# A layer norm's multiply moved from VectorE to GpSimd in a selective-scan kernel on one core

## The chip, the cores and the metric

The kernel runs on one core of a Trainium2 chip. The metric is the device time of one execution in microseconds. Before the change it is 16063.91 us, the median of three runs (16063.67 to 16070.08). In the profile, PE is TensorE's matrix unit and PEld its weight loads, DVE is VectorE, ACT is ScalarE, POOL is GpSimd and SP is the queue that issues nearly all DMAs.

## What is computed

Two blocks follow each other on a float32 tensor of 32 images, 96 channels and 56 x 56 positions. The first is a depthwise 7 x 7 convolution, a norm over the channels, two dense layers with a GELU between them, and a residual. The second is a pair of selective-scan layers over the 3136 positions of an image, then a batch norm over all images. Cut to the core of one layer of the second block:

```python
mu = seq.mean(-1); var = ((seq - mu) ** 2).mean(-1)
h = (seq - mu) * rsqrt(var + EPS) * ln_g + ln_b
xs, z = split(h @ in_w)
xc = silu(sum(conv_w[:, k] * shifted(xs, k) for k in range(4)) + conv_b)
dt, Bm, Cm = split(xc @ xproj_w)
delta = softplus(dt @ dt_w + dt_b)
state[t] = exp(delta * A) * state[t-1] + delta * Bm * xc     # 192 channels x 16 states
y = sum_s(state * Cm) + Dp * xc
seq = seq + (y * silu(z)) @ out_w
```

The change concerns the second line: the product with 1/sqrt(var + EPS). The mean is taken out by the weights that are prepared once, so the product is formed from seq itself and one row of 1/sqrt per position, the same in all 96 partitions.

## The kernel before

The 3136 positions of an image are four chunks of 784, and a chunk of a layer is one stage: 32 x 4 x 2 = 256 stages. Layer 0 of chunk n+1 and layer 1 of chunk n alternate. A stage has 24 steps (`NSTEP`): six groups j of 32 channels x 4 states over the partitions, times four state groups g. Each step is one scan on VectorE over 784 or 785 positions (`scan`, L959). For four of the six groups (j = 0, 1, 3, 4) VectorE also multiplies the scan's input from u and B (`times_b`, L887), four products per group; for groups 2 and 5 GpSimd does it (`pooled`, L941). After every second scan GpSimd multiplies the two states by C (L964), and TensorE adds them up into y (`add_up`, L1005) with L997 for the D term. VectorE multiplies y by the gate z (`gate`, L980) three times a stage. ScalarE forms exp(delta * A) ahead of each scan (`exps`, L904 and L905), and copies the carried states (L973). TensorE spreads u over the partitions (`spread`, L931), with a few matmuls without use before it, set by `FILL` (`keep_warm`, L917).

Between the steps stand pieces of other work: preparing the next stage (`prep`), finishing the last (`post`), half a chunk of the first block for an image further on (`block0`), and convolution taps for a later image (`conv`, seven taps, L552). The order is written out by hand. Each piece has a slot number: its integer part is the step after whose scan it is put, counted from the stage's start, and the fraction orders the pieces of one step. A piece marked `True` goes ahead of the scan's own products instead. Every engine, and SP, executes its instructions in exactly the order that comes of this (`manual_schedule`); waits on other engines are put in where data or buffers demand them.

In `prep`, the norm of the next stage is made thus. TensorE centres the chunk in two halves of 392 (L371), ScalarE squares them (L376), TensorE takes the mean over the channels (L381), and ScalarE turns it into 1/sqrt by a logarithm and an exponential (`rsqrt`, L387 and L388), in place in PSUM. VectorE then multiplies seq by that row of PSUM into the halo tile `hn` (L611, `norm(a)`, once per half), which has one buffer per layer and three columns of the previous chunk ahead of the 784 (`halo`, L604; at an image's first chunk a memset, L610). TensorE's projections L625 read hn. `product` (L707) on GpSimd is u = delta * xc, which VectorE's products and GpSimd's pooled ones use. `post` holds the output projection (L786, L792) and ScalarE's move of it into seq (L800, L806). In `block0`, the half-stage norm is made in the same way and multiplied by VectorE at L435.

The tiles that tie the engines together: hn, one per layer; h, seven buffers, written by a scan or a pooled product, multiplied by GpSimd and released by `add_up`; d4 (delta spread), three buffers, loaded by SP; us, one; two PSUM tiles `w` of two banks each for u and the exponentials; three PSUM tiles `ps` of one bank for everything else.

Of the kernel before, what the change touches and what calls it, by code (L numbers as in the profile page):

```python
# [36 lines left out]
AF = mybir.ActivationFunctionType  # L37
ALU = mybir.AluOpType
# [6 lines left out]
C = 96  # L45
# [7 lines left out]
CH = L // NCH  # L53
HC = CH // 2
# [7 lines left out]
def convnext_mamba_kernel(  # L62
# [31 lines left out]
    nc = tc.nc  # L94
# [29 lines left out]
    for dh in range(7):  # L124
# [3 lines left out]
            out=m, in_=ones, compare_op=ALU.is_equal, fill=0.0, base=3 - dh,  # L128
# [203 lines left out]
    hns, hn0s = [], []  # L332
# [13 lines left out]
    with ExitStack() as main:  # L346
# [12 lines left out]
        def tok(a):  # L359
            return slice(a * HC, (a + 1) * HC)  # L360
# [20 lines left out]
            nc.tensor.matmul(ps[0:C, 0:HC], mean_m, sq, start=True, stop=True)  # L381
            return ps

        def rsqrt(ps):

            rs = ps[0:C, 0:HC]
            nc.scalar.activation(rs, rs, AF.Ln, bias=eps_c[0:C])  # L387
            nc.scalar.activation(rs, rs, AF.Exp, scale=-0.5)  # L388

        batch_bias = {}
        batch_sums = {}

        def block0(b, c, s):
            k = c * 2 + s
            v = {}  # L400

            def load():
                if k == 0:
                    batch_sums[b] = work([C, NCH * 2], "sums", 2)
                v["cv"] = work([C, ROWS, W], "cv", 1)
                g = 0 if b < b0 else 1 + (b - b0) // NB
                at = (b - groups[g][0]) * W
                nc.sync.dma_start(
                    v["cv"],
                    conv_d[g].rearrange("(c h) w -> c h w", h=H)[  # L410
                        :, k * ROWS : (k + 1) * ROWS, at : at + W
                    ],
                )

            def load_x():
                v["xin"] = work([C, HC], "xin", 1)
                nc.sync.dma_start(v["xin"], x[b, :, k * HC : (k + 1) * HC])

            def center():
                v["cv"] = v["cv"].rearrange("p r w -> p (r w)")  # L420
                v["ps"] = centred(v["cv"], 2)

            def square():
                v["sq"] = squared(v["ps"])

            def mean():
                v["ps"] = mean_of(v["sq"], 2)

            def root():
                if pre and s == 0:  # L430
                    exp_ln_tables()
                rsqrt(v["ps"])

            def norm():
                nc.vector.tensor_tensor(hn0s[s][0:C], v["cv"], v["ps"][0:C, 0:HC], ALU.mult)  # L435

            def up():
                v["pss"] = [psum(f) for f in range(NF)]
                for f in range(NF):
                    nc.tensor.matmul(  # L440
                        v["pss"][f][:, 0:HC], w1_sb[:, f * 128 : (f + 1) * 128], hn0s[s],
                        start=True, stop=True,
                    )

            def gelu():
                v["gl"] = work([128, NF, HC], "gl", 1)
                for f in range(NF):
                    nc.scalar.activation(
                        v["gl"][:, f], v["pss"][f][:, 0:HC], AF.Gelu, bias=b1_sb[:, f : f + 1]
                    )  # L450
                if not pre:
                    exp_ln_tables()

            def down():
                v["ps"] = psum(2)
                nc.tensor.matmul(
                    v["ps"][0:C, 0:HC], eye, v["xin"], start=True, stop=False
                )
                for f in range(NF):
                    nc.tensor.matmul(  # L460
                        v["ps"][0:C, 0:HC], w2_sb[:, f, :], v["gl"][:, f, :],
                        start=False, stop=(f == NF - 1),
                    )

            def residual():
                nc.scalar.activation(
                    v["xin"], v["ps"][0:C, 0:HC], AF.Identity, bias=b2ls,
                    accum_out=batch_sums[b][:, k : k + 1],
                )
                nc.sync.dma_start(x1_d[b][:, k * HC : (k + 1) * HC], v["xin"])  # L470


            def total():
                v["m"] = work([C, 1], "mean", 2)
                nc.vector.tensor_reduce(v["m"], batch_sums[b], AX.X, ALU.add)

            def pool():
                ps = psum(0)
                nc.tensor.matmul(ps[0:C, 0:1], gpw_sb, v["m"], start=True, stop=True)
                v["gp"] = work([C, 1], "gp", 2)  # L480
                nc.scalar.activation(v["gp"], ps[0:C, 0:1], AF.Relu, bias=gpb, scale=1.0 / L)

            def fuse():
                ps = psum(1)
                nc.tensor.matmul(ps[0:C, 0:1], fw2, v["gp"], start=True, stop=True)
                fb = (
                    const.tile([C, 1], F32, name="fb0")
                    if pre
                    else wp.tile([C, 1], F32, name="fb", tag="fb", bufs=3)
                )  # L490
                nc.scalar.activation(fb, ps[0:C, 0:1], AF.Identity, bias=fusb)
                batch_bias[b] = fb

            last = [(21.5, total), (29.4, pool), (30.4, fuse)] if k == 2 * NCH - 1 else []
            return last + [
                (-6, load), (2, load_x), (11.2, center), (11.9, square), (12.4, mean),
                (12.6, root), (14.1, True, norm), (15.6, up), (15.8, gelu), (17.3, down),
                (18, residual),
            ]


# [34 lines left out]
        def conv(g, p):  # L536
# [11 lines left out]
            def tap(dw):  # L548
                def piece():
                    if dw == 0:  # L550
                        v["ps"] = psum(2)
                    nc.tensor.matmul(  # L552
                        v["ps"][0:R2, 0 : NB * W], v["band"][:, dw, :], xpad[:, :, dw : dw + W],
                        start=(dw == 0), stop=(dw == 6),
                    )

                return piece
# [5 lines left out]
                )  # L563
                nc.sync.dma_start(conv_d[g][p * R2 : (p + 1) * R2, :], t)

            at = (5.9, 6.1, 7.8, 8.6, 9.2, 9.6, 10.4)
            return [(-1, load), (10.5, store), *[(at[dw], tap(dw)) for dw in range(7)]]


        POOLED = (2, 5)  # L570
        AHEAD = {(2, 0): 0, (2, 1): 4.4, (5, 0): 12.3, (5, 1): 16.9}
        seqs = {}

        class Stage:
# [2 lines left out]
        def prep(S):  # L577
# [18 lines left out]
                v["ps"] = [mean_of(v["sq"][a], a) for a in range(2)]  # L596

            def root():
                for a in range(2):
                    rsqrt(v["ps"][a])  # L600

            def halo():
                if c > 0:
                    nc.scalar.copy(hns[i][:, 0:3], hns[i][:, CH : CH + 3])  # L604

            def norm(a):
                def piece():
                    hn = v["hn"] = hns[i]
                    if c == 0 and a == 0:
                        nc.vector.memset(hn[:, 0:3], 0.0)  # L610
                    nc.vector.tensor_tensor(  # L611
                        hn[0:C, 3 + a * HC : 3 + a * HC + HC], S.seq[:, tok(a)],
                        v["ps"][a][0:C, 0:HC], ALU.mult,
                    )

                return piece

            def project(q, weights, taps_, first, last):
                def piece():
# [110 lines left out]
            def load_d4(j):  # L730
# [8 lines left out]
            wx, wz = d["wx"], d["wz"].unsqueeze(1)  # L739
            start = [  # L740
                (-18, load), (-12.3, center), (-11.9, square), (-12.1, halo), (-11.6, mean),
                (-11.2, root), (-9, True, norm(0)), (-8.5, True, norm(1)),
            ]
            t = (-4.5, -4.4, -5.3, -4.8, -4, 0.2, 1.3, 2.3, 2.9, 3.4, 4)
            if S in (stages[2], stages[-1]):

                start = [
                    (10.3, center), (10.4, square), (10.5, halo), (10.9, mean), (11, root),
                    (12, norm(0)), (12, norm(1)),
                ]  # L750
                t = (12, 12, 13, 13, 14, 14, 15, 16, 17, 18, 19)
            elif S is stages[3]:

                start = [
                    (-18, load), (-4.5, center), (-4.4, square), (-4.3, halo), (-3.5, mean),
                    (-3, root), (-2, norm(0)), (-2, norm(1)),
                ]
                t = (0, 0, 0.1, 0.2, 0.3, 1, 2, 3.3, 4.1, 4.4, 5)
            t = [k + 0.1 for k in t]
# [7 lines left out]
                (max(10, t[8] + 1.2), load_bc(0, 0)), (max(10.2, t[8] + 1.2), load_bc(1, 0)),  # L767
                (max(16.8, t[8] + 2.2), load_bc(1, 1)), (max(19.8, t[8] + 2.2), load_bc(0, 1)),
                (t[9], dt), (t[10], softplus),
                (max(14, t[10] + 1.5), product), (max(18.3, t[10] + 3.1), store_u(0)),  # L770
                (25.3, store_u(1)),
                (max(16.5, t[10] + 2), load_d4(0)), (max(21.9, t[10] + 3), load_d4(1)),
                (max(20.3, t[10] + 3.2), load_u(0)), (23, load_d4(2)),
                (26, load_d4(3)), (32.9, load_u(1)), (30, load_d4(4)), (34, load_d4(5)),
            ]

        def post(S):
# [53 lines left out]

            pieces = [(7.9, project), (8.9, move(0)), (9.2, move(1))]
            if i == 1:
                pieces += [(12.7, save), (17.2, stat(0)), (19, stat(1))]
            return pieces


# [3 lines left out]
        LAG = 4  # L841
        LAG0 = 4
        KS = 2
        FILL = {0: 4, 4: 12}
        GATES = (5, 13, 20)
        SPREADS = [(21, 0), (27, 1), (34, 3), (38, 4)]
        WS = ((0, 3), (1, 2), (), ())
# [323 lines left out]
```

## Time and profile before

The profiled execution took 16065.38 us and its span, from the first instruction to the last, is 16063.7 us.

| engine | busy, us | share of the span |
|---|---|---|
| VectorE (DVE) | 15341.8 | 96% |
| GpSimd (POOL) | 13950.6 | 87% |
| TensorE (PE) | 13868.6 | 86% |
| ScalarE (ACT) | 11941.9 | 74% |

| group | count | busy, us | mean, ns |
|---|---|---|---|
| scans, L959 (both kinds) | 6144 | 10683.5 | 1769 and 1775 |
| GpSimd, state times C, L964 | 3072 | 9968.7 | 3249 |
| GpSimd, pooled products, L941 | 1024 | 3318.0 | 3240 |
| VectorE, products with B, L887 | 4096 | 3906.1 (2916.0 + 990.1) | 980 and 967 |
| GpSimd, u, L707 | 256 | 685.6 | 2678 |

Some 560 us before the loop go to the convolution of the first images and to weights, and some 360 us after it to the batch norm's pass over DRAM; the stages lie between. Durations in a row are start to end of one instruction. Neighbouring instructions of an engine overlap a little, so what an instruction costs its engine is the distance from its start to the start of the next. A line with `[1.04 <-DVE h L959]` says that the engine was idle for 1.04 us before it and that the scan at L959 ended that. DVE, ACT and POOL rows are exact to some tens of ns, PE rows are modelled at their ends.

### The profile page before, as it was taken

The numbers are of one execution on the slowest core, as the hardware profiler recorded it, in microseconds if no ns is written. First come the engines' busy times: TensorE is split into PE (matmuls) and PEld (weight loads), VectorE is DVE, ScalarE is ACT, GpSimd is POOL, SyncE is SP. The second block draws the span as 40 slices with busy tenths as digits, with TensorE's granted clock in tenths as the row PEclk, the third lists the DMA queues.
The fourth block names the chain that finished last, engine by engine and source line by source line (L and its number), as shares of the span: only waits on it lengthen the run. The fifth ranks groups of instructions, "written<-read, shape, count | busy, mean of one in ns | idle before, by whom it ended". The sixth has DMA issues, their size and how long they took to land. (4 is left out here: it accounts for less than half of the span.)

```text
span 16063.7 us, 215150 instructions
## 1 busy us (share of the span) xinstructions
PE 13868.6 (86%) x74840; PEld 5981.5 (37%) x74840; DVE 15341.8 (96%) x12358; ACT 11941.9 (74%) x23139; POOL 13950.6 (87%) x4446
## 2 busy tenths in 40 slices
PE   8888988888988888888898888889888888888870
PEld 5333333333333333333333333333333333333330
DVE  8699999999999999999999999999999999999993
ACT  1577777777777777777777777777777777777763
POOL 1599999999999999999999999999999999999980
PEclk9899999999999999999999999999999999999985
DMA  4344444444444444444444444444444444444438
GB/s 112 110 148 147 149 149 146 149 147 149 150 146 149 147 149 150 146 149 147 148 150 146 148 148 148 149 146 148 147 148 139 136 138 137 138 139 139 138 123 293
DMA packets 1307226, 2362.65 MB, mean 147 GB/s; under 512 B 495918, under 2 KB 697914, under 8 KB 1306136
## 3 DMA queue, kind: packets, MB, share of 16 engines
q1 hardware_dynamic: 1296808, 2308.46, 47.0%
q10 hardware_dynamic: 7168, 38.54, 0.6%
q8 instruction: 590, 9.67, 0.2%
q14 instruction: 500, 4.10, 0.1%
q0 software_dynamic: 2160, 1.88, 0.1%
HBM read 1945.97 MB, written 402.41 MB: 146 GB/s over the span
## 5 line engine op out<-in xcount | busy, mean ns | idle before, releaser
L964 POOL TENSOR_TENSOR h<-h,cp 128x1568 f32<-128x1568 f32 x3072 | 9968.7, 3249 | 1177.4 <-DVE h L959 974.4
L959 DVE TENSOR_TENSOR_SCAN h<-w,h 128x785 f32<-128x785 f32 (+1 forms) x3072 | 5293.9, 1769 | 122.9 <-ACT w L905 110.1
L959 DVE TENSOR_TENSOR_SCAN h<-da,w 128x785 f32<-128x785 f32 (+1 forms) x3072 | 5389.6, 1775 | 2.6 <-ACT da L905 2.6
L941 POOL TENSOR_TENSOR h<-us,bp 128x1570 f32<-128x1570 f32 x1024 | 3318.0, 3240 | 56.3 <-PE y L1005 29.8
L905 ACT ACTIVATE w<-d,A 128x784 f32<-128x784 f32 x3072 | 2819.1, 918 | 671.3 <-DVE h L959 587.7
L887 DVE TENSOR_TENSOR w<-w,bp 128x786 f32<-128x786 f32 x3072 | 2916.0, 980 | 146.4 <-PE w L931 24.7
L905 ACT ACTIVATE da<-d,A 128x784 f32<-128x784 f32 x3072 | 2876.5, 947 | 12.7 <-DMA d<-dd 11.9
L1005 PE MATMUL y<-h,ssum 128*32 128x392 f32 x24576 | 2460.1, 511 | 79.5 <-POOL h L964 79.2
L625 PE MATMUL ps<-hn,wx 97*64 97x392 f32 x12288 | 2204.2, 500 | 9.1 <-DVE hn L611 9.1
L931 PE MATMUL w<-u,sel 64*128 64x393 f32 x4096 | 998.0, 562 | 1328.2 <-DVE h L959 1233.2
L904 ACT COPY w<-st 128x1 f32<-128x1 f32 x2304 | 371.6, 161 | 1510.9 <-DVE h L959 1473.4
L625 PEld LDWEIGHTS ps<-hn,wx 97*64 97x64 f32 x12288 | 814.8, 136 | 1331.2 <-issue 1296.6
L1005 PEld LDWEIGHTS y<-h,ssum 128*32 128x32 f32 x24576 | 662.4, 111 | 1643.5 <-issue 1416.8
L552 PE MATMUL ps<-xpad,band 112*112 112x280 f32 x2688 | 1032.5, 509 | 259.3 <-ACT dl L695 259.3
L707 POOL TENSOR_TENSOR u<-dl,xc 128x1176 f32<-128x1176 f32 x256 | 685.6, 2678 | 489.2 <-ACT dl L695 470.7
L917 PEld LDWEIGHTS y<-sel 128*128 128x128 f32 x8192 | 981.6, 193 | 253.2 <-issue 184.1
L917 PE MATMUL y<-sel 128*128 128x120 f32 x8192 | 1029.3, 279 | 14.6 <-DVE z L980 14.6
L887 DVE TENSOR_TENSOR h<-w,bp 128x786 f32<-128x786 f32 x1024 | 990.1, 967 | 0.0
L367 ACT ACT_TABLE_LOAD x759 | 973.8, 1283 | 14.2 <-PEq L1158 0.8
L931 PEld LDWEIGHTS w<-u,sel 64*128 64x128 f32 x4096 | 331.5, 190 | 1716.5 <-DVE h L959 980.6
L552 PEld LDWEIGHTS ps<-xpad,band 112*112 112x112 f32 x2688 | 490.2, 207 | 871.2 <-issue 450.6
L792 PE MATMUL ps<-z,ow 64*96 64x392 f32 x3072 | 797.1, 668 | 0.0
(158 smaller groups left out, 15917.6 us busy)
## 6 DMA issues: line engine op xcount, KB each, us to landing
d<-dd SPq DMA_DIRECT2D x1536, 392.0 KB, 3.6
bp<-bd SPq DMA_DIRECT2D x1024, 392.0 KB, 4.6
cp<-bd SPq DMA_DIRECT2D x1024, 392.0 KB, 6.0
us<-uu SPq DMA_DIRECT2D x512, 392.0 KB, 4.5
dd<-dl SPq DMA_DIRECT2D x512, 294.0 KB, 3.7
band<-band_d SPq DMA_DIRECT2D x192, 343.0 KB, 5.8
uu<-u SPq DMA_DIRECT2D x1024, 49.0 KB, 3.4
cv<-conv_d SPq DMA_DIRECT2D x256, 147.0 KB, 2.7
```

Of the source, the lines that this page charges most:

```text
L367: nc.scalar.preload_act_table_set("natural_log_exp_and_others")
L552: nc.tensor.matmul(v["ps"][0:R2, 0 : NB * W], v["band"][:, dw, :], xpad[:, :, dw : dw + W], start=(dw == 0), stop=(dw == 6),)
L625: nc.tensor.matmul(v["x", q][rows(a), 0:HC], weights[:, k, 64 * q : 64 * q + 64], v["hn"][:, o : o + HC], start=(k == 0), stop=(k == last),)
L792: nc.tensor.matmul(v["ps"][a][0:C, 0:HC], S.d["ow"][rows(a), q, :], S.z[rows(a), q, :], start=False, stop=(q == NQ - 1),)
L887: nc.vector.tensor_tensor(halves(S.pb[j, g]), halves(S.u4[j])[:, :, 0 : HC + 1], halves(S.bc[0, g // 2][:, g % 2, :]), ALU.mult,)
L905: nc.scalar.activation(e[:, 1 : 1 + CH], S.d4[j], AF.Exp, scale=S.d["A"][:, j, g : g + 1])
L917: nc.tensor.matmul(spare, sel[:, 0, :], sel.rearrange("p a b -> p (a b)")[:, 0 : 512 - HC], start=True, stop=True,)
L931: nc.tensor.matmul(u4[:, 512 * a : 512 * a + HC + 1], sel[rows(a), j % 2, :], S.u[rows(a), j // 2, a : a + HC + 1], start=True, stop=True,)
L941: nc.gpsimd.tensor_tensor(states(S, j, h)[:, :, 0 : 1 + CH], S.us[j].unsqueeze(1).broadcast_to([128, 2, 1 + CH]), S.bc[0, h][:, :, 0 : 1 + ...
L959: nc.vector.tensor_tensor_scan(h[:, g % 2, at], S.e.pop((j, g))[:, at], S.pb.pop((j, g), h[:, g % 2, :])[:, at], 1.0 if c else 0.0, ALU.mu ...
L964: nc.gpsimd.tensor_tensor(h[:, :, 0:CH], h[:, :, 1 : 1 + CH], S.bc[1, g // 2], ALU.mult)
L1005: nc.tensor.matmul(S.y[r0 : r0 + 32, 0:HC], ssum, hs[k][:, g, tok(a)], start=False, stop=(half == 1 and g == 1),)
```

## The change

`rsqrt` takes a destination. In `prep`, ScalarE's exponential writes 1/sqrt not back to PSUM but into the 784 columns of hn, and a single `norm` multiplies seq by them on GpSimd, in place in hn; the halo memset goes to GpSimd too. In `block0` the same could be chosen by `ZP`, which is 0: there the multiply stays on VectorE with PSUM as its input. The norm's slot is -9.5 (step 14 of the stage before) where the two VectorE multiplies stood ahead of step 15's products.

Slots of other pieces are set anew: in `block0` up, gelu and residual; the convolution's taps (the third from 7.8 to 8, which is behind the output projection at 7.9) and its store; the first pooled product; three of the projections; two stores of u; three loads of delta; the second statistic of layer 1. `FILL` for group 0 is 3 instead of 4.

```diff
-        def rsqrt(ps):
-            rs = ps[0:C, 0:HC]
-            nc.scalar.activation(rs, rs, AF.Ln, bias=eps_c[0:C])
-            nc.scalar.activation(rs, rs, AF.Exp, scale=-0.5)
+        def rsqrt(ps, out):
+            ln = ps[0:C, 0:HC]
+            nc.scalar.activation(ln, ln, AF.Ln, bias=eps_c[0:C])
+            nc.scalar.activation(out, ln, AF.Exp, scale=-0.5)
+        ZP = 0
...
-                rsqrt(v["ps"])
+                v["rs"] = hn0s[s][0:C] if ZP else v["ps"][0:C, 0:HC]
+                rsqrt(v["ps"], v["rs"])
             def norm():
-                nc.vector.tensor_tensor(hn0s[s][0:C], v["cv"], v["ps"][0:C, 0:HC], ALU.mult)
+                eng = nc.gpsimd if ZP and not pre else nc.vector
+                eng.tensor_tensor(hn0s[s][0:C], v["cv"], v["rs"], ALU.mult)
...
-                (12.6, root), (14.1, True, norm), (15.6, up), (15.8, gelu), (17.3, down),
-                (18, residual),
+                (12.6, root), ((14.1, norm) if ZP else (14.1, True, norm)), (15, up), (15.2, gelu), (17.3, down),
+                (17.7, residual),
...
-            at = (5.9, 6.1, 7.8, 8.6, 9.2, 9.6, 10.4)
-            return [(-1, load), (10.5, store), *[(at[dw], tap(dw)) for dw in range(7)]]
+            at = (5.7, 5.9, 8, 8.7, 9, 9.4, 10.2)
+            return [(-1, load), (10.3, store), *[(at[dw], tap(dw)) for dw in range(7)]]
-        AHEAD = {(2, 0): 0, (2, 1): 4.4, (5, 0): 12.3, (5, 1): 16.9}
+        AHEAD = {(2, 0): 0.5, (2, 1): 4.4, (5, 0): 12.3, (5, 1): 16.9}
...
             def root():
+                v["hn"] = hns[i]
                 for a in range(2):
-                    rsqrt(v["ps"][a])
+                    rsqrt(v["ps"][a], hns[i][0:C, 3 + a * HC : 3 + a * HC + HC])
...
-            def norm(a):
-                def piece():
-                    hn = v["hn"] = hns[i]
-                    if c == 0 and a == 0:
-                        nc.vector.memset(hn[:, 0:3], 0.0)
-                    nc.vector.tensor_tensor(
-                        hn[0:C, 3 + a * HC : 3 + a * HC + HC], S.seq[:, tok(a)],
-                        v["ps"][a][0:C, 0:HC], ALU.mult,
-                    )
-                return piece
+            def norm():
+                hn = v["hn"]
+                if c == 0:
+                    nc.gpsimd.memset(hn[:, 0:3], 0.0)
+                hn = hn[0:C, 3 : 3 + CH]
+                nc.gpsimd.tensor_tensor(hn, S.seq, hn, ALU.mult)
...
-                (-11.2, root), (-9, True, norm(0)), (-8.5, True, norm(1)),
+                (-11.2, root), (-9.5, norm),
-            t = (-4.5, -4.4, -5.3, -4.8, -4, 0.2, 1.3, 2.3, 2.9, 3.4, 4)
+            t = (-4.5, -4.4, -5.8, -4.8, -4.2, 0.2, 1.3, 2.3, 2.9, 3.4, 4)
...
-                (max(14, t[10] + 1.5), product), (max(18.3, t[10] + 3.1), store_u(0)),
-                (25.3, store_u(1)),
-                (max(16.5, t[10] + 2), load_d4(0)), (max(21.9, t[10] + 3), load_d4(1)),
-                (max(20.3, t[10] + 3.2), load_u(0)), (23, load_d4(2)),
-                (26, load_d4(3)), (32.9, load_u(1)), (30, load_d4(4)), (34, load_d4(5)),
+                (max(14, t[10] + 1.5), product), (max(17.1, t[10] + 3.1), store_u(0)),
+                (29, store_u(1)),
+                (max(18.1, t[10] + 2), load_d4(0)), (max(21.9, t[10] + 3), load_d4(1)),
+                (max(20.3, t[10] + 3.2), load_u(0)), (24, load_d4(2)),
+                (26.9, load_d4(3)), (32.9, load_u(1)), (30, load_d4(4)), (34, load_d4(5)),
...
-                pieces += [(12.7, save), (17.2, stat(0)), (19, stat(1))]
+                pieces += [(12.7, save), (17.2, stat(0)), (18.7, stat(1))]
...
-        FILL = {0: 4, 4: 12}
+        FILL = {0: 3, 4: 12}
```

In three special stages (the third, the fourth and the last) the norm is put at a slot of its own, 12 or -2, in one piece where it was two.

More of the change, by code (lines that the diff above doesn't have):

```diff
@@ L748, in prep @@
                     (10.3, center), (10.4, square), (10.5, halo), (10.9, mean), (11, root),
-                    (12, norm(0)), (12, norm(1)),
+                    (12, norm),
                 ]
@@ L755, in prep @@
                     (-18, load), (-4.5, center), (-4.4, square), (-4.3, halo), (-3.5, mean),
-                    (-3, root), (-2, norm(0)), (-2, norm(1)),
+                    (-3, root), (-2, norm),
                 ]
```

## The prediction

> **What bounds the kernel now.** First the busy times of the engines, then a stretch of 1000 us from the middle (columns: length, busy time and instructions of PE, PEld, DVE, ACT, POOL, granted clock, DMA share, GB/s):
>
> ```profile
> PE 13868.6 (86%) x74840; PEld 5981.5 (37%) x74840; DVE 15341.8 (96%) x12358; ACT 11941.9 (74%) x23139; POOL 13950.6 (87%) x4446
> ```
>
> ```profile
> 8000.00:9000.00 1000.00, 895.45 (x4925) 387.43 (x4918) 983.46 (x786) 782.12 (x1533) 920.61 (x289) 0.95 0.48 147
> ```
>
> VectorE leaves 1.7% free in the stage loop and GpSimd 8%. What VectorE still waits for, from the waits of DVE between 815 and 14864 us:
>
> ```profile
> DVE h L959 <- ACT w L905: 95.6, 70, 2.0
> DVE z L980 <- PE y L1005: 13.1, 11, 1.2
> DVE h L959 <- ACT st L973: 12.7, 9, 2.0
> ```
>
> That is about 125 us in 14,050: the loop runs at VectorE's own issue rate, and what leaves VectorE shortens it if GpSimd can keep up. The chain that ended last holds only the closing pass over DRAM, so it says nothing of the loop. I read a stage from the timeline instead (start, duration, instruction); this stage starts at 6542.50, the next 58.5 us later. VectorE, then GpSimd:
>
> ```profile
> 6576.86 1.78 DVE L959 TENSOR_TENSOR_SCAN h<-da,w 128x785 f32<-128x785 f32 x1
> 6578.56 0.55 DVE L611 TENSOR_TENSOR hn<-seq,ps 96x392 f32<-96x392 f32 x1
> 6579.04 0.55 DVE L611 TENSOR_TENSOR hn<-seq,ps 96x392 f32<-96x392 f32 x1
> 6579.51 1.78 DVE L959 TENSOR_TENSOR_SCAN h<-w,h 128x785 f32<-128x785 f32 x1
> ```
>
> ```profile
> 6576.57 3.23 POOL L964 TENSOR_TENSOR h<-h,cp 128x1568 f32<-128x1568 f32 x1 [1.04 <-DVE h L959]
> 6579.85 2.68 POOL L707 TENSOR_TENSOR u<-dl,xc 128x1176 f32<-128x1176 f32 x1
> 6582.48 3.27 POOL L964 TENSOR_TENSOR h<-h,cp 128x1568 f32<-128x1568 f32 x1
> 6585.70 3.26 POOL L941 TENSOR_TENSOR h<-us,bp 128x1570 f32<-128x1570 f32 x1
> 6588.89 6.50 POOL L964 TENSOR_TENSOR h<-h,cp 128x1568 f32<-128x1568 f32 x2
> 6595.89 6.62 POOL L964 TENSOR_TENSOR h<-h,cp 128x1568 f32<-128x1568 f32 x2 [0.50 <-DVE h L959]
> ...
> 6617.43 6.53 POOL L964 TENSOR_TENSOR h<-h,cp 128x1568 f32<-128x1568 f32 x2 [1.18 <-DVE h L959]
> ```
>
> VectorE issues without a hole across the two norms; GpSimd has holes ended by scans, so it follows VectorE (left out between the last two rows: L941 at 6602.47, two L964 from 6606.43, L941 at 6613.03). Adjacent engine instructions overlap in these rows: a norm lasts 0.55 but costs VectorE 6579.51 - 6578.56 = 0.95 us for two.
>
> **What the skill says.** *GPSIMD Engine Reference*, "3.1 Elementwise": a two-input float32 add of 2048 elements takes 4497 ns there, 2.2 ns an element. The trace agrees: 3249/1568 = 2.07 (L964), 2678/1176 = 2.28 (L707). *SBUF — State Buffer*, "Who interferes with whom": VectorE contends with a reading GpSimd operation only where it has two SBUF inputs or a 2-port mode. In this loop scans, L887, gates and norms each have one operand in PSUM; the scan lasts 1758 to 1792 ns whatever GpSimd does, so the trace shows no such loss, and the change adds no VectorE instruction with two SBUF inputs. *TensorE: Matmul & The Clock Gate*, "What's actually happening": the clock falls to half after a quiet window of about 3.4 us, free-running. The trace agrees on the half: 0.57 mean over the twelve microseconds quoted under the slots below.
>
> **The change part by part.** (1) Removed from VectorE: two norms in each of 256 stages, 0.95 us by the two rows' starts (the halo memset of 0.06 lay inside them). Between the scans nothing else is waited for: L964, L887 and the exps for the next scans are earlier in their queues, so the next scan moves up. 256 x 0.95 = 243 us off.
>
> (2) Added to GpSimd: one multiply of 784 elements. No row has this size; bounds 784 x 2.07 = 1.62 and 784 x 2.28 = 1.79, the page gives 1.72. I take 1.7; a fixed cost might make it 2.1. For 64 stages a memset of three columns, under 0.1. In GpSimd's new order it stands behind the product u (L707) and ahead of the h multiply of scan 15. Queue by queue: product ends 6582.5, norm 6584.2, then 3.22 us each: L964 6587.4, L941 6590.65, L964 6593.9, 6597.1, 6600.35, 6603.6, L941 6606.8, L964 6610.0 and 6613.3, L941 6616.5. The next multiply waited for its scan until 6617.43 and is due 0.95 earlier, at 6616.48: the backlog is gone there, and if the norm took 2.1 the 1.04 us hole before scan 13's multiply would take the rest. GpSimd's sum rises from about 54.1 to 55.8 us of a stage of 57.55. Full, but it closes.
>
> Who waits meanwhile: the TensorE sum y of scan 15 (L1005) began at 6588.21 and needs the multiply that now ends at 6587.4 instead of 6585.7: still in time. Its sum ends at 6589.73 and VectorE's gate z, at 6591.82 now, is due at 6590.87: 1.1 us of cover where there were 2.1. The projection L625 that reads hn starts at 6586.74, two microseconds after the new hn. Pooled products (L941) are read four or more scans later; of the seven h buffers, the scan that takes one freed by a multiply comes ten us or more after it.
>
> (3) ScalarE writes 1/sqrt to SBUF, not PSUM: *ScalarE: Activation LUTs*, "Step-by-step: what each stage is for", calls PSUM the faster destination. The nearest rows are 474 ns (L388, to PSUM) and 487 (L376, to SBUF): 0.03 us a stage on an engine with 22% free, hidden. A gain: the PSUM tile is freed by ScalarE and not by VectorE. The half-stage norm keeps its place on VectorE, since ZP is 0.
>
> (4) Where the stall goes. After the norms VectorE runs 0.95 early against TensorE and ScalarE, which are tied again only by the scan before the u spread (L931). The 11 + 9 stages which already wait at the gate or for a state gain nothing: 20 x 0.95 = 19 us back; as many again I count as near it: 39 us lost, between 0 and 80.
>
> (5) Slots. One of the four fill matmuls before the first spread goes: 0.29 us of TensorE; the gap there (fill ends 6596.24, spread 6597.58, after its scan) shrinks from 1.34 to 0.39 + 0.29, so it costs nothing. Loads and stores are the same in number and size; the d, u and cp moves stay behind or before the same waits of SP, with several us until their readers. One convolution tap (L552) goes behind the output projection (L786, L792). The 70 waits above, 1.37 us each, stand there; one such stage (from 6836.41), TensorE, ScalarE, VectorE, and the clock:
>
> ```profile
> 6851.04 1.25 PE L552 MATMUL ps<-xpad,band 112*112 112x280 f32 x2
> ...
> 6855.44 4.24 PE L792 MATMUL ps<-z,ow 64*96 64x392 f32 x12
> ```
>
> ```profile
> 6859.71 0.49 ACT L800 ACTIVATE seq<-ps 96x392 f32<-96x392 f32 x1 [2.69 <-PE ps L792]
> 6860.10 0.91 ACT L905 ACTIVATE w<-d,A 128x784 f32<-128x784 f32 x1
> ```
>
> ```profile
> 6861.11 3.47 DVE L959 TENSOR_TENSOR_SCAN h<-w,h 128x784 f32<-128x784 f32 x2 [1.68 <-ACT w L905]
> ```
>
> ```profile
> 6848.40:6860.40 12.00, 10.96 (x28) 4.58 (x28) 11.03 (x9) 5.96 (x12) 10.53 (x5) 0.57 0.40 117
> ```
>
> The projection runs at half clock, ScalarE's move queues behind it and the exp behind the move. The removed tap is 1.25 us of that path: at most 70 x 1.1 = 77 us gained; but which stages meet the slow window moves with the new period, so I take 40, bounds -80 (a loss) to 77.
>
> Sum: 243 - 39 + 40 = 244 us. The profiled execution took 16065.38 us with a span of 16063.7; the median of the runs is 16063.91, one and a half under it, so the difference is taken from the median: 15820.
>
> **The rivals.** *GpSimd becomes the bound* (the slower side). At about 97% it has little room; if the norm lasted long, the multiply of scan 15 would hold the y sum, the gate at 6590.87 would stall VectorE, and the lag would not be gone a stage later. For the sum to be late, the norm has to take 1.7 + 0.8 = 2.5 us; to eat the 1.1 us of cover, 3.6; to eat the saved 0.95 as well, 4.5. At 5 us a stage loses 0.5: 16190. Against it: both rows per element. *The clock takes it back*: with the tap and the fill gone, every stage instead of 70 meets the long slow stretch: 256 x 1.37 - 96 = 255 us, against 243 - 39 saved: 16115; if half of the stages do, 16063.9 - 204 + 80 = 15940. For it: the clock falls in both kinds of stage; against it: total TensorE work is unchanged but for the fill. *Waits move in*: ScalarE's exps or TensorE keep the old period where VectorE had cover under 0.95, in half of the stages: 122 saved, 15940. *The slots give more*: the waits at the projection go and nothing is lost: 243 + 90, 15730. That the change does not do what it says is excluded for order: the two VectorE multiplies are gone in each stage's list and the GpSimd one stands in it.
>
> **How the numbers follow.** Forecast (15740 to 15890) 0.70; waits move in or the clock takes half (15890 to 16030) 0.16; slots give more (under 15740) 0.07; clock takes all or GpSimd bounds 0.07, of which 0.03 ends within 0.2% (32 us, about what a measurement can tell from no change) and 0.04 above. Faster 0.93, same 0.03, slower 0.04. The range reaches into the moved waits above and over the slots' 15730 below: 15725 to 15930 leaves out 0.05 below and 0.14 above.
>
> **What would show it.** Right: scan to scan across the old norm at 1.7 us; stage period near 57.6; GpSimd near 92 to 93% busy with a row of 784 elements at 1.6 to 1.8 us; its waits for scans down from 974 us; no growth of VectorE's waits for y. Wrong: the gate waiting for y in most stages (GpSimd late), or DVE's waits for the exp well over 100 us (clock, or ScalarE).

## The result, and the profile after

The changed kernel takes 15843.72 us (median of four runs, 15834.59 to 15851.25) against 16064.51 us for the kernel before: a ratio of 0.9862, 95% interval 0.9845 to 0.9879. That is 221 us off; the forecast was 15820, 244 off. The profiled execution took 15850.69 us with a span of 15848.7.

From the page of the changed kernel: the busy time of its engines, GpSimd's costliest group, and from further down the groups the new row:

```profile
PE 13987.3 (88%) x74328; PEld 5953.8 (38%) x74328; DVE 15121.7 (95%) x11782; ACT 11958.4 (75%) x23139; POOL 14379.5 (91%) x4766
...
L963 POOL TENSOR_TENSOR h<-h,cp 128x1568 f32<-128x1568 f32 x3072 | 9938.5, 3251 | 548.4 <-DVE h L958 467.0
...
L615 POOL TENSOR_TENSOR hn<-seq,hn 96x784 f32<-96x784 f32 x256 | 478.1, 1868 | 462.3 <-ACT hn L388 455.4
```

VectorE has 576 instructions fewer (512 norms, 64 memsets) and GpSimd 320 more. VectorE's busy time falls by 220 us, the span by 215. GpSimd's waits for scans fall from 974 to 467 us: it has used half of its holes. The 455 us at L615 are its one long wait before the stages begin, not a cost of the norm. Line numbers are one lower than before in most of the loop.

The waits of VectorE in the stage loop (us in total, times, longest), of the changed kernel between 815 and 14655 us:

```profile
DVE h L958 <- ACT w L904: 88.2, 102, 2.6
DVE w L886 <- PE w L930: 18.5, 67, 0.9
DVE h L958 <- ACT st L972: 3.7, 7, 1.1
```

About 114 us in 13,840, much as before: VectorE still sets the loop. Now the stage that the prediction walked, in the changed kernel; it starts at 6449.30. VectorE's timeline at the old place of the norms, and GpSimd's from scan 13's multiply on (start, duration, instruction):

```profile
6483.94 1.78 DVE L958 TENSOR_TENSOR_SCAN h<-da,w 128x785 f32<-128x785 f32 x1
6485.64 1.76 DVE L958 TENSOR_TENSOR_SCAN h<-w,h 128x785 f32<-128x785 f32 x1
```

```profile
6483.65 3.24 POOL L963 TENSOR_TENSOR h<-h,cp 128x1568 f32<-128x1568 f32 x1 [1.03 <-DVE h L958]
6486.94 2.68 POOL L706 TENSOR_TENSOR u<-dl,xc 128x1176 f32<-128x1176 f32 x1
6489.55 0.10 POOL L613 MEMSET hn<- 97x3 f32 x1
6489.61 1.87 POOL L615 TENSOR_TENSOR hn<-seq,hn 96x784 f32<-96x784 f32 x1
6491.44 3.25 POOL L963 TENSOR_TENSOR h<-h,cp 128x1568 f32<-128x1568 f32 x1
6494.63 3.27 POOL L940 TENSOR_TENSOR h<-us,bp 128x1570 f32<-128x1570 f32 x1
6497.85 12.92 POOL L963 TENSOR_TENSOR h<-h,cp 128x1568 f32<-128x1568 f32 x4
6510.69 3.29 POOL L940 TENSOR_TENSOR h<-us,bp 128x1570 f32<-128x1570 f32 x1
```

Scan to scan is 1.70 us where it was 2.65. GpSimd now runs the second half of the stage without a hole, and the hole of 1.03 us ahead of scan 13's multiply is still there, so the backlog does end within each stage.

To see where the rest went, I averaged the distance from one scan's start to the next over the 238 stages from the fifth on, step by step, from the same scan rows of the two traces:

| up to scan | what lies there | before, us | after, us | over 238 stages |
|---|---|---|---|---|
| 15 | the norms; exp for scan 15 | 2.631 | 1.744 | 211 gained |
| 10 | exp queued behind the projection's move | 2.165 | 1.964 | 48 gained |
| 20 | the second gate | 2.199 | 2.141 | 14 gained |
| 3 | exp after the gate's SiLU | 1.682 | 1.768 | 20 lost |
| 19 | exp behind the residual | 1.679 | 1.805 | 30 lost |
| 12 | spread of u after group 2 | 3.654 | 3.701 | 11 lost |

All other steps differ by less than 4 us over these stages. All 24 steps together are 211 us, within 4 of the spans' difference.

### The profile page after: what moved, and what is told of

Its sections match the earlier page's. It is cut to its first block, busy times and chain, and to the rows that moved or that the text cites. A ratio compares the mean times of both kernels' runs of the same rounds, so it can differ in the third digit from the quotient of the medians.

```text
span 15848.7 us, 213573 instructions
## 1 busy us (share of the span) xinstructions
PE 13987.3 (88%) x74328; PEld 5953.8 (38%) x74328; DVE 15121.7 (95%) x11782; ACT 11958.4 (75%) x23139; POOL 14379.5 (91%) x4766
## 5 line engine op out<-in xcount | busy, mean ns | idle before, releaser
L963 POOL TENSOR_TENSOR h<-h,cp 128x1568 f32<-128x1568 f32 x3072 | 9938.5, 3251 | 548.4 <-DVE h L958 467.0
L1004 PE MATMUL y<-h,ssum 128*32 128x392 f32 x24576 | 2590.9, 511 | 59.2 <-POOL h L963 59.2
L555 PE MATMUL ps<-xpad,band 112*112 112x280 f32 x2688 | 909.8, 458 | 284.0 <-ACT dl L694 284.0
L916 PEld LDWEIGHTS y<-sel 128*128 128x128 f32 x7680 | 920.0, 192 | 251.2 <-DVE h L958 113.7
L916 PE MATMUL y<-sel 128*128 128x120 f32 x7680 | 967.5, 279 | 12.1 <-DVE z L979 12.1
L615 POOL TENSOR_TENSOR hn<-seq,hn 96x784 f32<-96x784 f32 x256 | 478.1, 1868 | 462.3 <-ACT hn L388 455.4
L791 PE MATMUL ps<-z,ow 64*96 64x392 f32 x3072 | 849.2, 706 | 0.0
L555 PEld LDWEIGHTS ps<-xpad,band 112*112 112x112 f32 x2688 | 437.6, 186 | 868.0 <-ACT dl L694 402.6
```

Source lines behind the costliest of these rows:

```text
L555: nc.tensor.matmul(v["ps"][0:R2, 0 : NB * W], v["band"][:, dw, :], xpad[:, :, dw : dw + W], start=(dw == 0), stop=(dw == 6),)
L791: nc.tensor.matmul(v["ps"][a][0:C, 0:HC], S.d["ow"][rows(a), q, :], S.z[rows(a), q, :], start=False, stop=(q == NQ - 1),)
L916: nc.tensor.matmul(spare, sel[:, 0, :], sel.rearrange("p a b -> p (a b)")[:, 0 : 512 - HC], start=True, stop=True,)
L963: nc.gpsimd.tensor_tensor(h[:, :, 0:CH], h[:, :, 1 : 1 + CH], S.bc[1, g // 2], ALU.mult)
L1004: nc.tensor.matmul(S.y[r0 : r0 + 32, 0:HC], ssum, hs[k][:, g, tok(a)], start=False, stop=(half == 1 and g == 1),)
```

## The experiments

Each was timed beside the kernel before (medians 16060 to 16069 us). Diffs are cut to the lines that matter. Where a wait "at scan n" has a sum in us, it is VectorE's idle time ahead of that scan over the same 238 stages.

**The move alone, on the old slots.** The two norms go to GpSimd as in the change; every other slot, and the fill, stay as before. Of the edit, the slot (the code of the norm is that of the change):

```diff
-                (-11.2, root), (-9, True, norm(0)), (-8.5, True, norm(1)),
+                (-11.2, root), (-9.5, norm),
```

> The move alone, on the slots of the kernel before. Theory (the two VectorE multiplies are the gain, the slots decide only small waits): 16064 - 0.89 x 256 = 15836, plus the waits for the exp of scan 10 that the third tap ahead of the projection leaves (some 50 us): 15850 to 15900; scan 14 to scan 15 at 1.7 us. Rival (the slots carry a good part, since GpSimd and the queues fit only with them): over 15950.

Measured 15834.78 us (15826.72 to 15842.49), ratio 0.9860, interval 0.9844 to 0.9877: the whole gain, and nothing that can be told from the changed kernel. The rival falls. The first theory holds in that the two multiplies are the gain, but the time is below its range: it added 50 us of waits at scan 10 to a time of 16064 that already held 108 of them. These fell here too, to 69 us, with the third tap still ahead of the projection. The new slots were not needed for GpSimd to fit.

**The slots alone.** The changed kernel with the norms back on VectorE, PSUM as their input.

```diff
-                (-11.2, root), (-9.5, norm),
+                (-11.2, root), (-9, True, norm(0)), (-8.5, True, norm(1)),
```

> The new slots alone, the norm left to VectorE with PSUM as its input. Theory: VectorE still issues the same work, so only the waits for the exp of scan 10 shrink, 108 to about 57 us over the middle stages: 16064 - 50 = 16014, between 15990 and 16050. Rival (the slots are worth much by themselves): below 15980.

Measured 16092.68 us, ratio 1.0021 (1.0012 to 1.0030): slower than both expectations. The waits at scan 10 did fall, to 49 us, but 86 us appeared at scan 3, in 75 stages. TensorE's timeline around the stage change of one such stage (the ninth; the first scan at 1045.86):

```profile
1042.46 1.28 PE L934 MATMUL w<-u,sel 64*128 64x393 f32 x4 [1.51 <-DVE h L962]
1043.67 2.83 PE L628 MATMUL ps<-hn,wx 97*64 97x392 f32 x8
1046.43 0.93 PE L1000 MATMUL y<-xc,D 128*128 128x392 f32 x2
```

After a gap of 1.51 us the projection L628 takes 2.83 us instead of 1.54: the granted clock is 0.50 from 1042.90 to 1046.32, and what follows on ScalarE, up to the exp of scan 3, is late. The suspect is the missing fill matmul.

**The same with four fill matmuls.**

```diff
-        FILL = {0: 3, 4: 12}
+        FILL = {0: 4, 4: 12}
```

> The new slots alone with the norm left on VectorE, but four fill matmuls ahead of the first spread again instead of three. Theory (with the old period the missing fill lets TensorE's clock fall behind it, which delays the gate's SiLU and the exp of scan 3): the 85 us of waits at scan 3 go, about 16010. Rival (another slot does it, the moved loads for one): 16090, the waits at scan 3 stay.

Measured 16023.11 us, ratio 0.9972 (0.9962 to 0.9983). The wait at scan 3 is 3 us, and the same stage's place is at full clock:

```profile
1045.18 0.93 PE L934 MATMUL w<-u,sel 64*128 64x393 f32 x4 [1.29 <-DVE h L962]
1046.04 1.54 PE L628 MATMUL ps<-hn,wx 97*64 97x392 f32 x8
```

So the fill did it. One matmul less ahead of the spread costs 70 us at the old period, and nothing that shows at the new one, where VectorE's scan ends the gap 0.94 us earlier: the median gap before this spread is 1.53 us in the slots alone, 1.31 with four fills and 0.59 in the changed kernel. The length of the gap does not decide alone. In the slots alone it was 1.45 us or more in 219 of the 238 stages, and the clock fell in 75 of them; these 75 are exactly the stages that wait at scan 3. With four fills it fell in one stage, in the changed kernel in none. The other slots are worth about 40 us at the old period; with the norm moved they are worth nothing.

**The in-place multiply on VectorE.**

```diff
-                nc.gpsimd.tensor_tensor(hn, S.seq, hn, ALU.mult)
+                nc.vector.tensor_tensor(hn, S.seq, hn, ALU.mult)
...
-                (-11.2, root), (-9.5, norm),
+                (-11.2, root), (-9, True, norm),
```

> The changed kernel with the in-place multiply on VectorE, one instruction of 784 elements with both inputs in SBUF. If VectorE keeps its rate of about 1.2 ns an element beside GpSimd (0.95 us), the time is that of the slots alone, about 16015. If two SBUF inputs make it wait for the GpSimd instruction under way, a multiply of about 3.2 us, each stage loses up to that: 16100 to 16850, and the row's time or the gap at that place shows it.

Measured 16608.34 us, ratio 1.0342 (1.0327 to 1.0358). One stage of it, VectorE and then GpSimd:

```profile
6783.94 2.08 DVE L615 TENSOR_TENSOR hn<-seq,hn 96x784 f32<-96x784 f32 x1
```

```profile
6781.95 3.24 POOL L963 TENSOR_TENSOR h<-h,cp 128x1568 f32<-128x1568 f32 x1 [1.04 <-DVE h L958]
6785.23 3.33 POOL L706 TENSOR_TENSOR u<-dl,xc 128x1176 f32<-128x1176 f32 x1
```

The multiply starts 1.25 us before GpSimd's L963 ends, and ends 0.83 us after that: 2.08 us, where the shortest of the 256 took 0.97. GpSimd's next, which starts while VectorE's multiply is still under way, takes 3.33 us instead of 2.68. That is the contention of two SBUF inputs which *SBUF — State Buffer*, "Who interferes with whom", states, and its cost here: scan 14 to scan 15 becomes 3.69 us, 1.06 more than with two PSUM multiplies, or 253 us of the 516 against the slots alone. Most of the rest, 206 us, lies at scan 3, where the waits are 286 us against 86. That is the clock again: VectorE reaches the scan ahead of the spread 1.06 us later, the median gap on TensorE grows from 1.53 to 2.60 us, and the clock falls in 138 stages, which are exactly those that wait at scan 3. So with 1/sqrt in SBUF the multiply could not have stayed on VectorE without this loss.

**The multiply left out, and a second one put in.** Two kernels that change GpSimd's load alone. The first leaves out the product with seq, so its output is not the norm; it only shows what the multiply costs.

```diff
-                nc.gpsimd.tensor_tensor(hn, S.seq, hn, ALU.mult)
```

> The changed kernel without the multiply (hn keeps 1/sqrt alone; the multiply by seq is left out of the computation): neither VectorE nor GpSimd does it. Theory (GpSimd's backlog holds the y sum of scan 21 and with it the exp of scan 3, 0.09 us a stage): scan 2 to scan 3 returns from 1.77 to 1.68 us, 15844 - 22 = 15820. Rival (GpSimd's share is free, hidden as the prediction had it): 15844, within 5 us. Rival (the backlog costs more than at scan 3): below 15800.

Measured 15831.91 us (15815.70 to 15834.88), ratio 0.9855. Scan 2 to scan 3 is back at 1.68 us in every stage, as the first theory has it: 21 us of VectorE's time. The waits at scan 10 rose by 21 us in the same stages, and the whole is 12 us, which the intervals of the two kernels do not tell from nothing. So what is shown is the 0.09 us a stage at scan 3: the norm at its new place costs the kernel some 21 us at most, of the 478 that GpSimd spends on it.

```diff
+                nc.gpsimd.tensor_tensor(hn, hn, one.broadcast_to([C, CH]), ALU.mult)
                 nc.gpsimd.tensor_tensor(hn, S.seq, hn, ALU.mult)
```

> The changed kernel with a second GpSimd multiply of 784 elements (hn by a column of ones, in place) ahead of the norm: 1.87 us more of GpSimd in each stage, the output is unchanged. Theory (what GpSimd carries beyond the present backlog falls through the y sum of scan 21 onto scan 3, nearly whole): scan 2 to scan 3 grows by about 1.9 us, 15844 + 256 x 1.9 = 16330, between 16250 and 16400. Rival (GpSimd only has to fit in the stage, 57.8 us of sum plus holes of 0.6): 58.5 us a stage, about 15990. Rival (hidden): 15844.

Measured 16250.42 us, ratio 1.0116 (1.0101 to 1.0131). GpSimd, and VectorE at scan 3, in one stage (scan 3 comes 33 us ahead of these multiplies, and waits for what the stage before left over):

```profile
6662.53 1.50 POOL L618 TENSOR_TENSOR hn<-hn,one 96x784 f32<-96x784 f32 x1
6664.11 1.86 POOL L619 TENSOR_TENSOR hn<-seq,hn 96x784 f32<-96x784 f32 x1
```

```profile
6629.42 1.79 DVE L962 TENSOR_TENSOR_SCAN h<-w,h 128x785 f32<-128x785 f32 x1 [1.56 <-ACT w L908]
```

With the broadcast operand the extra multiply is 1.50 us and not the 1.87 of my expectation. The lag of GpSimd behind scan 15 grows by 1.57 us, and scan 2 to scan 3 by 1.46, to 3.23: nearly all of it lands on VectorE, with the mechanism expected, and both rivals fall. GpSimd's whole load would still have fitted in 58.5 us; it is not its sum that bounds, but the one multiply whose reader is near. The changed kernel stands just at the edge.

**The slots around the small waits.** First the residual back behind the exp of scan 19:

```diff
-                (17.7, residual),
+                (18, residual),
```

> The changed kernel with the residual of the first block back at slot 18, behind the exp for scan 19. Theory (at 17.7 it stands ahead of that exp, and in the late stages without convolution it waits for a slow TensorE): the 28 us of waits at scan 19 go, the gate's waits of 13 to 16 us come back, so about 15830. Rival (the waits only move to other places): 15844 within 5.

Measured 15845.63 us, ratio 0.9864, as the rival had it. The theory was right about the wait and wrong about the gain. In the changed kernel one late stage reads on ScalarE and VectorE:

```profile
13474.29 0.58 ACT L469 ACTIVATE xin<-ps,b2ls 96x392 f32<-96x392 f32 x1 [1.99 <-PE ps L463]
...
13475.05 0.92 ACT L904 ACTIVATE w<-d,A 128x784 f32<-128x784 f32 x1
```

```profile
13476.00 1.79 DVE L958 TENSOR_TENSOR_SCAN h<-w,h 128x785 f32<-128x785 f32 x1 [2.58 <-ACT w L904]
```

The residual waits for TensorE, the exp stands behind it, and the scan waits for the exp. With the slot back these 28 us are gone, and 22 come at the gate behind the same late TensorE. One wait took the other's place.

Then, with that slot kept, fill matmuls in the late stages, which have no convolution:

```diff
+            elif m >= 2:
+                put(m, [(k, lambda: keep_warm(3)) for k in (5.7, 5.9, 8, 8.7)])
```

> As the one before, and in the 62 late stages without convolution twelve fill matmuls at steps 5 to 8 in the taps' place. Theory (the late stages wait because TensorE's clock falls where the taps are missing): the waits at scans 15 and 19 and at the gate in those stages fall from about 50 us to under 20, 15800 to 15820. Rival (the clock falls at another place of the stage): no change against the one before, about 15830.

Measured 15852.12 us, ratio 0.9869: no gain. The wait at scan 15 went (5 us to 0), the gate's rose from 22 to 31. Twelve fills at that place raise the clock behind them and not where it matters: from the 195th stage on, its mean over scans 10 to 12 is 0.99 instead of 0.85, and over scans 15 and 16 it is 0.79 instead of 0.90.

The third tap back ahead of the projection:

```diff
-            at = (5.7, 5.9, 8, 8.7, 9, 9.4, 10.2)
+            at = (5.7, 5.9, 7.8, 8.7, 9, 9.4, 10.2)
```

> The changed kernel with the third convolution tap back ahead of the output projection. Theory (the tap is 1.25 us of the slow path to the exp of scan 10): the waits at scan 10 rise from 57 to about 110 us, 15844 + 50 = 15895. Rival (with the new period it matters little, since the kernel with the move alone has 69 us there): 15844 to 15860.

Measured 15848.77 us, ratio 0.9863; the waits at scan 10 are 62 us against 57. The rival holds: the tap is worth nothing at this period. The 11 us at scan 12 come back, and 14 more are lost at scan 15.

Last, an attempt at what is left. ScalarE's two moves of the projection go behind the exp of scan 10; once in the changed kernel, and once on the old slots with the move alone, where the third tap is put at 8 too.

```diff
-            pieces = [(7.9, project), (8.9, move(0)), (9.2, move(1))]
+            pieces = [(7.9, project), (9, move(0)), (10, move(1))]
```

> The changed kernel with ScalarE's two moves of the output projection at slots 9 and 10, behind the exp for scan 10 and the exps for scan 11. Theory (the waits at scan 10 are the exp queued behind a move that waits for TensorE): they fall from 57 to under 20 us, 15844 - 40 = 15805. Rival (the wait goes to scan 11, or to the next norm's centring): 15835 to 15850.

> The move alone on the slots of the kernel before, with the third tap behind the projection and the two moves at slots 9 and 10. Theory: the 69 us at scan 10 fall to under 20, 15835 - 50 = 15785. Rival: 15825 to 15840.

Measured 16076.14 us (ratio 1.0006) and 16335.67 us (1.0166). The waits at scan 10 are zero in both, as the theory had it, and yet 232 and 500 us were lost. Theory and rival both miss: the loss is many times the rival's, and it does not come through the next norm's centring, which in the first kernel starts 29.5 us into the stage, as in the changed one (medians). It is the square behind it that is late. ScalarE's waits there, in the first kernel and in the second, and one of them:

```profile
ACT sq L376 <- DMA conv_d<-sq: 227.7, 93, 4.4
```

```profile
ACT sq L376 <- DMA conv_d<-sq: 476.5, 187, 4.7
```

```profile
6314.15 0.49 ACT L376 ACTIVATE sq<-ps 96x392 f32<-96x392 f32 x1 [2.40 <-DMA conv_d<-sq]
```

The squares and the convolution's output share the tile `sq`, which has three buffers. In these kernels the norm's last square gets the buffer that the convolution's store (issued at 6308.19 in this stage, landed at 6314.05) is still reading; in the changed kernel and with the move alone no square waits for that store. The waits amount to nearly the whole loss. Behind the square come the roots, the half-stage norm (L438) and the exps. In the first kernel only every second stage has this wait. From scan 11 to the next stage's scan 11 these take 60.62 us instead of 57.98, and the others, with the same two moves, 58.03 instead of 58.13 (means of the stages with convolution); the late stages without convolution lose nothing either. Why the slots of two moves change which buffer is handed out was not followed, and a fourth buffer for `sq` was not tried. No version that I ran clearly beats the changed kernel; the move alone, 15834.78 us, is level with it.

## Why the prediction was right

The bound and the mechanism held: what leaves VectorE shortens the stage. Step by step:

1. *Removed from VectorE*, 243 us by one stage's rows. The medians of scan 14 to scan 15 are 2.62 and 1.70 us, 0.926 x 256 = 237. The walked stage had a memset besides the norms; the size was near enough.

2. *Added to GpSimd*, 1.7 us, ends 1.62 and 2.1. It measured 1.87: more per element than either row (2.38 ns against 2.28 and 2.07), as with the fixed cost that it allowed for, and inside the ends. The walk said that scan 15's multiply would end 44.9 us after the stage's start, and it ended at 45.39; that the backlog would be gone by the multiply of scan 5, and the median lag there is 0.14 us; that the hole of 1.04 us ahead of scan 13 would stay, and 1.03 is there. The y sum of scan 15 started after its multiply, and the gate did not wait for it in the middle stages. Of the signs, the row at 1.6 to 1.8 us and the busy share of 92 to 93% were missed by a little (1.87 us, 91%), and the stage's median is 57.92 us where 57.6 was said.

3. *The step that failed* is "Who waits meanwhile". It named the y sum of scan 15 and stopped. The y sum of scan 21 runs at the stage change, where the backlog still is 2.4 us. TensorE before and after, at the start of the stage (6542.50 before, 6449.30 after), before first:

```profile
6542.28 1.52 PE L1005 MATMUL y<-h,ssum 128*32 128x392 f32 x16
6543.74 2.20 PE L625 MATMUL ps<-hn,wz 97*64 97x392 f32 x12
```

```profile
6449.08 2.15 PE L1004 MATMUL y<-h,ssum 128*32 128x392 f32 x16
6451.16 2.20 PE L624 MATMUL ps<-hn,wz 97*64 97x392 f32 x12
```

The sum takes 2.15 us instead of 1.52, since the weight loads of its second half wait 0.49 us for GpSimd's multiply. The projection of z comes 0.62 us later, ScalarE's SiLU behind it, and then the exp of scan 3. ScalarE and VectorE before, then after:

```profile
6548.10 0.92 ACT L905 ACTIVATE w<-d,A 128x784 f32<-128x784 f32 x1
```

```profile
6549.47 1.76 DVE L959 TENSOR_TENSOR_SCAN h<-w,h 128x785 f32<-128x785 f32 x1
```

```profile
6455.41 0.92 ACT L904 ACTIVATE w<-d,A 128x784 f32<-128x784 f32 x1
```

```profile
6456.36 1.79 DVE L958 TENSOR_TENSOR_SCAN h<-w,h 128x785 f32<-128x785 f32 x1
```

The exp had ended 0.45 us ahead of its scan; now the scan starts 0.03 us after it. Counted from the stage's start, the exp is 0.51 us later, against 0.45 of cover: scan 3 is 0.09 us later in this stage, and as much in the mean, 20 us over the middle stages. Leaving the norm out gave this back; a second multiply sent nearly its whole length down the same path.

4. *Where the stall goes*, 39 us lost. The waits at scans 15, 19 and 12 amount to 10 (within the first row of the table), 30 and 11 us, less 14 gained at the gate: about 37. The size was right, in part by luck: the places were partly others, since the residual's new slot traded the gate's wait for one at scan 19.

5. *Slots*, 40 us gained at scan 10, bounds -80 and 77. It measured 48, and that is luck, since the reason given fails at the new period: putting the tap back changes the waits there by 5 us, and the move alone on the old slots lost 40 of the 108 us. At the old period the slots alone bring them to 49; whether the tap does it there was not tested. Which stages meet the half clock is not something that I could read ahead. The fill was read rightly: it costs nothing because the gap shrinks, to 0.59 us where the prediction said 0.68. What it did not say is that at the old period the same matmul is worth 70 us.

With the measured sizes the sum is 237 - 20 - 37 + 48 = 228 us, against 221 measured. One reading was a little narrow: scans last 1757 to 1796 ns over both kinds, not 1758 to 1792; nothing rests on it.

The rivals: GpSimd as the bound comes true with one more multiply (16250), at 1.5 us more. The prediction had put the point at which the whole saving is eaten 2.8 us above its 1.7, because it watched the gate and not scan 3. The clock is real, as the slots alone show. Before it fell in the stage shown there, TensorE had been busy for 1.90 of 3.41 us, so the window of about 3.4 us that the prediction cites as quiet need not be a wholly idle one. In the changed kernel it did not fall at the stage change; around scans 5 to 8 it was lower than before (0.66 in the mean instead of 0.72), but the waits at scan 10, behind that stretch, fell all the same. Waits that move in took part of the gain, not half.

## What to carry to other kernels

When work goes to an engine that still has holes, walk its queue through the stage with the new instruction in it, and at every multiply that ends later ask for its nearest reader, round the stage's end too: the sum of the busy times said that GpSimd fits, and the one reader that was missed cost 0.09 us a stage, and about 1.5 us more when one more instruction was put in. A slot that removes a wait often hands it to the next piece in the same queue: each of the single slots tried here moved its wait without gain, or lost. A slot can also change which buffer a later instruction gets, so read the name of the wait before explaining a loss. And the fill matmul here was worth 70 us at one period and nothing at another: its worth has to be measured again when the period changes.

## What the runs showed of the hardware

A GpSimd multiply of two float32 SBUF operands took 1868 ns for 784 elements, 2683 for 1176 and 3251 for 1568, so in these three the time per element falls with the length; with one operand a broadcast column, 784 elements took 1494. A VectorE multiply with both operands in SBUF took 2078 ns in the median beside a busy GpSimd and 971 at its shortest, and the GpSimd product behind it grew from 2683 to 3383 ns. ScalarE's exponential of 392 elements took 493 ns into SBUF and 474 into PSUM. TensorE's gap before the first spread, over 238 stages each of six kernels (before, changed, move alone, slots alone, the same with four fills, multiply on VectorE in SBUF): below 1.45 us it was followed by half clock in none of 983 stages, from 1.45 to 1.7 us in 73 of 221, from 1.7 to 2.4 us in 3 of 14, and above that in 138 of 210. What decides between stages with the same gap stays open.
